# One max and one subtraction for two layers, and a semantic product in 32-row tiles: two cross-attention layers on one Trainium2 core

## The chip, the cores and the metric

The kernel runs on one NeuronCore of a Trainium2 chip. The metric is device time in microseconds (us), and less is better. All data are fp32. The engines are TensorE (PE; its weight loads are shown apart as PEld), VectorE (DVE), ScalarE (ACT), GpSimd (POOL) and SyncE (SP), which issues nearly all DMAs.

## The reference

Two cross-attention layers follow each other over 64 batch rows of 256 tokens and 320 channels, with 20 heads of 16 channels. The context has 77 rows of 512 channels; in layer 1 the last four of them are image rows. Cut to what matters:

```python
# layer 0: ip is empty (TEXT_LEN = 77)
q, k, v = split_heads(x @ Wq.T), split_heads(ctx @ Wk.T), split_heads(ctx @ Wv.T)
x = x + (softmax(q k^T / 4) v) @ Wo.T + bo

# layer 1: 73 text rows, 4 image rows
probs_t  = softmax(q k_t^T / 4)                       # [b, h, s, 73]
text_out = probs_t @ v_t
qsem     = l2norm(probs_t @ text_rows)                # 512 channels per head and token
sem      = qsem @ l2norm(ip_rows)^T                   # [b, h, s, 4]
probs_ip = softmax(q k_ip^T / 4 + 0.5 * sem) * spatial_mask
x = x + (text_out + probs_ip @ v_ip) @ W_out + b_out
```

## The kernel before

**No 512-channel intermediate.** With unnormalized weights w of layer 1, the kernel uses the Gram matrix G of the context rows. One product of w with [G | G times the image rows | values | 1] gives, for a head and a token, 94 columns: 73 of w G, 4 image sums, 16 text outputs and the sum of w. The squared norm of qsem is then w times (w G), summed. This is the *semantic product* (`semantics`, L774 and L781).

**Units.** The batch rows are taken in pairs p (32 pairs). A pair has ten units: for each of its two rows b five units, each of which is eight head slots of 128 tokens (four quarters r of 32 channels, two heads e in each). The main loop runs over g; g // 10 is p and g % 10 is k, the place in the pair. In one g, layer 0's scores of unit g and layer 1's scores of unit g - 13 are made, and the semantic product of the layer 1 unit of the g before. Layer 1 of a row thus runs while layer 0 of the next pair does. 307 values of g have both layers, the first 13 layer 0 alone and the last 13 layer 1 alone; 320 have a semantic product.

**One PSUM tile per g.** `ps` (tag `sc`) takes four of the eight PSUM banks, one bank for each quarter r, in one buffer. A bank holds layer 0's scores, layer 1's scores and the semantic product. So the first matmul of the next g (L774) waits until everything of this g has been read out of `ps`.

**The order inside one g,** as each engine gets it. PE, ACT, DVE and POOL keep the order in which the program is written (`keep_order`, from g = 13 on):

1. evictions of query or output projections held from the g before (`drains`): ACT L602 or L945, DVE L617; then PE: semantic product (L774, L781), scores of both layers (L659);
2. `shifted` for layer 0, then for layer 1: DVE max over the text (L677), DVE subtraction into `w` (L679);
3. `transposed(1)` of the g before: PE L723, L724; ACT L730, L731;
4. `exponential(0)`: ACT L687 on layer 0's `w`, except at k = 5, where it stands behind step 7;
5. DVE `weighted` (L792, L795): the semantic product times the weights;
6. `first` fillers: key, value or output projections, the Gram matrix and others, with their evictions on ACT (L348 `kT`, L391 `vs`, L516 and L517 `gram`, L589 `q`);
7. `transposed(0)` of the g before: PE L723, L724; ACT L749, L750, or L738, L741 in the last unit of a row;
8. `sums_out` (ACT L1057): the remaining 21 columns out of `ps`; at k = 1 and 6 it stands ahead of step 7;
9. `exponential(1)`: ACT L690, L691, and POOL L694, which copies the image scores from `w`; `normalize`: DVE L705, L706, POOL L710;
10. DVE L1130 and, at the end of a row, a chain of small steps (L870, L871, L844 and others);
11. `second` fillers, `attend` at four of the ten k (PE L809, L814, at k = 0, 2, 5, 7), `third` fillers.

Small PSUM tiles come from two pools of two buffers each: `ptr` (tag `tr`: transposes, `itr` L915, `ltr`, one `pv`) and `pms` (tag `ms`: projections, keys, values, Gram, the other `pv`). A matmul into such a tile waits until ACT or DVE has emptied the tile that had the buffer before it.

**The right-hand side of the semantic product.** `gv[b]` holds, for three channel groups and four blocks, G's first 64 rows twice (two halves of 64 partitions) and the values beside it; `gr[b]` holds the remaining nine rows in four quarters. `gram` fills `gram` and `g_rest` with one and eight DMAs, `place_gram` (POOL L530, L534) copies them into place. `values` fetches value rows from DRAM (`v_rows`) by DMA, `place_values` (POOL L435, L441, L449, L455 for layer 1; L464, L470, L475 for layer 0) places them.

Of the kernel before, what the change touches and what calls it, by code (L numbers as in the profile page):

```python
# [21 lines left out]
TT = T - NIP  # L22
P = 128
# [47 lines left out]
def tile_two_cross_attentions(ctx: ExitStack, tc: tile.TileContext, a: dict, out: bass.AP):  # L71
# [202 lines left out]
    gv = [const.tile([P, 3, 4, GV], F32, tag=f"gv{b}", name=f"gv{b}") for b in range(2)]  # L274
    gr = [const.tile([P, 3, 2, GR], F32, tag=f"gr{b}", name=f"gr{b}") for b in range(2)]
    for b in range(2):
        nc.vector.memset(gv[b][:, :, :, GV - 1 :], 1.0)
        nc.vector.memset(gr[b], 0.0)
        nc.gpsimd.tensor_copy(
            gr[b][:, :, :, GR - 1 :], rest1.unsqueeze(1).unsqueeze(3).broadcast_to([P, 3, 2, 1])  # L280
        )
# [5 lines left out]
    v_rest = [const.tile([P, C], F32, tag=f"v_rest{b}", name=f"v_rest{b}") for b in range(2)]  # L287
# [3 lines left out]
    parts1 = [const.tile([P, 5, 2, M], F32, tag=f"parts1{i}", name=f"parts1{i}") for i in range(3)]  # L291
# [45 lines left out]
    def keys(l, p, i):  # L337

        nt = (T, TT)[l]
        if i == 0:  # L340
            kTs[l] = big.tile([P, 2, 2, T], F32, tag=f"kT{l}", name=f"kT{l}_{p}", bufs=1)
# [8 lines left out]
    def last_keys(p):  # L350
# [5 lines left out]
        for l in range(2):  # L356
            nt = (T, TT)[l]
            kl = kls[l, p] = big.tile([P, 2, T], F32, tag=f"kl{l}", name=f"kl{l}_{p}", bufs=1 + l)
# [6 lines left out]
    def place_image_keys(p):  # L365

        k = kipT[:, :, 2 * p * NIP : 2 * (p + 1) * NIP].rearrange("p i (b t) -> p i b t", b=2)
        nc.gpsimd.tensor_copy(kTs[1][:, :, :, TT:], k[:, :2])
        nc.gpsimd.tensor_copy(kls[1, p][:, :, TT:], k[:, 2])

    def keys_by_head(l, p, b):

        kbd = kbds[l, b] = big.tile([P, 3, 2, T], F32, tag=f"kbd{l}", name=f"kbd{l}_{p}_{b}")
        for i, k in ((slice(0, 2), kTs[l][:, :, b, :]), (slice(2, 3), kls[l, p][:, b : b + 1, :])):
            full = [P, k.shape[1], 2, T]
# [7 lines left out]
    def value_rows(i, l):  # L383
# [8 lines left out]
        if l:  # L392
            v_rows[i] = dram.tile([P, 2, C], F32, tag="v_rows", name=f"v_rows{i}", bufs=8)
            nc.sync.dma_start(v_rows[i][:n], stage[i][:n])
# [3 lines left out]
    def from_rows(to, l, p, b, t0, t1):  # L398
# [3 lines left out]
        while at < end:  # L402
            i, r = divmod(at, P)
            n = min(P - r, end - at)
            o = at - r0 - t0
            nc.sync.dma_start(to[o : o + n, :], v_rows[i][r : r + n, l, :])
# [6 lines left out]
    def values(l, p, b):  # L413

        nt = (T, TT)[l]
        rem = nt - M
        vm = small.tile([P, C], F32, tag="vm", name=f"vm{l}_{p}_{b}", bufs=1)
        vr = v_rest[b] if l else small.tile([8 * rem, C], F32, tag="vr", name=f"vr{p}_{b}", bufs=1)
        for e in range(2):
            from_rows(vm[e * M : (e + 1) * M, :], l, p, b, 0, M)  # L420
        for i in range(8):
            r = i // 2 * QR + i % 2 * rem if l else i * rem
            from_rows(vr[r : r + rem, :], l, p, b, M, nt)
        fetched[l] = (vm, vr)

    def place_values(l, p, b):
# [3 lines left out]
        if l:  # L430

            for j in range(2):
                rows = slice(j * M, (j + 1) * M)
                for part in range(2):
                    nc.gpsimd.tensor_copy(  # L435
                        gv[b][rows, part, :, T : T + D].rearrange("p (e a) d -> p e a d", e=2),
                        vm[rows, 8 * D * part : 8 * D * (part + 1)].rearrange(
                            "p (a j e d) -> p j e a d", a=2, j=2, e=2
                        )[:, j],
                    )  # L440
                nc.gpsimd.tensor_copy(  # L441
                    gv[b][rows, 2, :, T : T + D].rearrange("p (e a) d -> p e a d", e=2),
                    vm[rows, HT * D + j * QR : HT * D + (j + 1) * QR]
                    .rearrange("p (e d) -> p e d", e=2).unsqueeze(2).broadcast_to([M, 2, 2, D]),
                )
            for r in range(4):
                rows = slice(r * QR, (r + 1) * QR)
                full = [QR, 2, 2, D]
                nc.gpsimd.tensor_tensor(  # L449
                    gr[b][rows, :2, :, T - M : T - M + D],  # L450
                    vr[rows, : HT * D].rearrange("p (i r e d) -> p r i e d", i=2, r=4, e=2)[:, r],
                    rest1[rows].unsqueeze(1).unsqueeze(3).broadcast_to(full), ALU.mult,
                )
                c0 = HT * D + r % 2 * QR
                nc.gpsimd.tensor_tensor(  # L455
                    gr[b][rows, 2, :, T - M : T - M + D], vr[rows, c0 : c0 + QR].rearrange("p (e d) -> p e d", e=2),
                    rest1[rows].unsqueeze(2).broadcast_to([QR, 2, D]), ALU.mult,
                )
# [42 lines left out]
    grams = {}  # L501

    def gram(p, b):
# [10 lines left out]
        g = small.tile([P, T], F32, tag="gram", name=f"gram{p}_{b}", bufs=2)  # L514
# [6 lines left out]
        nc.sync.dma_start(g[M:, :], g[:M, :])  # L521
# [4 lines left out]
        grams[b] = g  # L526

    def place_gram(b):
        g, gx = grams[b], g_rest[b]
        nc.gpsimd.tensor_copy(  # L530
            gv[b][:, :, :, :T], g.unsqueeze(1).unsqueeze(1).broadcast_to([P, 3, 4, T])
        )
# [116 lines left out]
    SEM0 = 4 * T  # L649

    def scores(ps, start, stop, l, p, b, u):
# [4 lines left out]
        for r in range(4):  # L656
            rows = slice(r * QR, (r + 1) * QR)
            for c in halves_of(P):
                nc.tensor.matmul(  # L659
                    ps[c, r, 2 * T * l : 2 * T * (l + 1)], tokens[rows, c],  # L660
                    kbd[rows, part].rearrange("p e t -> p (e t)"), start=start, stop=stop,
                )

    def shifted(ps, l, p, b, u):

# [538 lines left out]
```

## Time and profile before

| | |
|---|---|
| Time of three runs | median 2474.22 us (2473.43 to 2474.65) |
| Profiled execution | 2474.45 us, span 2472.7 us |
| Granted TensorE clock | 0.999 |
| Busy | PE 97%, PEld 75%, DVE 80%, ACT 60%, POOL 55% |
| DMA | 131.83 MB in 150914 packets, mean 53 GB/s |
| First and last semantic product | 114.9 us and 2444.0 us into the span |
| `L677` max, layer 0 / layer 1 | 796 / 756 ns each, x320 each |
| `L679` subtraction | 800 ns, x640 |
| `L774` semantic product, 64x64 tiles, 94 columns | 277.9 us busy, x10240 |
| `L659` scores, 32x64 tiles, 154 columns | 247.7 us busy, x10240 |

The profile shows one execution. An fp32 matmul is recorded as two matmul instructions, so a unit's 16 matmuls of L774 are 32 records. Matmuls on different tiles of the array overlap, and the time of a group is therefore the union of its records. The idle time given beside a row is the engine's idle time just before it, with whoever ended most of it. PE being busy includes matmuls that stand behind one another.

### The profile page before, as it was taken

The numbers are of one execution on the slowest core, as the hardware profiler recorded it, in microseconds if no ns is written. First come the engines' busy times: TensorE is split into PE (matmuls) and PEld (weight loads), VectorE is DVE, ScalarE is ACT, GpSimd is POOL, SyncE is SP. The second block draws the span as 40 slices with busy tenths as digits, with TensorE's granted clock in tenths as the row PEclk, the third lists the DMA queues.
The fourth block names the chain that finished last, engine by engine and source line by source line (L and its number), as shares of the span: only waits on it lengthen the run. The fifth ranks groups of instructions, "written<-read, shape, count | busy, mean of one in ns | idle before, by whom it ended". The sixth has DMA issues, their size and how long they took to land.

```text
span 2472.7 us, 100470 instructions
## 1 busy us (share of the span) xinstructions
PE 2394.2 (97%) x41118; PEld 1847.9 (75%) x41118; DVE 1987.4 (80%) x3673; ACT 1482.2 (60%) x3767; POOL 1370.9 (55%) x3483
## 2 busy tenths in 40 slices
PE   7899999999999999999999999999999999999888
PEld 5677777777777777777777777777777777777676
DVE  3588788888888888888888888888888888888864
ACT  3466666666666666666665666665665666666543
POOL 2455565566555656555656555556555556555542
PEclk9999999999999999999999999999999999999999
DMA  6212111112111112111121211121211121211000
GB/s 173 75 30 57 50 52 47 56 53 58 52 57 41 54 54 59 52 52 51 47 59 56 62 45 48 46 60 56 62 44 48 47 59 56 61 39 39 26 23 25
DMA packets 150914, 131.83 MB, mean 53 GB/s; under 512 B 45432, under 2 KB 129144, under 8 KB 150456
## 3 DMA queue, kind: packets, MB, share of 16 engines
q1 hardware_dynamic: 149592, 124.27, 17.5%
q8 instruction: 325, 5.32, 0.9%
q10 hardware_dynamic: 864, 1.15, 0.2%
q14 instruction: 133, 1.09, 0.1%
HBM read 87.43 MB, written 33.91 MB: 49 GB/s over the span
## 4 chain that ended last, share of the span: by engine, by line
PE 76%; DVE 12%; ACT 3%; DMA 3%; POOL 2%; issue 1%; SPq 1%; DVEq 0%; POOLq 0%; ACTq 0%
PE tr L723 10%; PE sc L774 9%; PE o_ps L547 8%; PE q_ps L547 8%; PE sc L659 7%; DVE w L679 5%; PE v_ps L390 4%; PE sc L781 4%; PE o_ps L632 3%; DVE mx L677 3%; PE k_ps L345 3%; PE pv L809 2%; PE q_ps L557 2%; PE o_ps L557 2%; PE q_ps L575 2%; PE pv L814 2%
## 5 line engine op out<-in xcount | busy, mean ns | idle before, releaser
L677 DVE TENSOR_REDUCE mx<-sc 128x8 f32<-128x584 f32 (+1 forms) x640 | 496.6, 776 | 342.1 <-PE sc L659 339.3
L710 POOL TENSOR_TENSOR parts<-w,sm 128x512 f32<-128x512 f32 (+1 forms) x640 | 440.6, 709 | 437.1 <-DVE sm L706 144.2
L679 DVE TENSOR_TENSOR w<-sc,mx 128x616 f32<-128x616 f32 x640 | 511.8, 800 | 73.0 <-DVE mx L677 1.4
L723 PE MATMUL tr<-ident,parts 128*128 128x128 f32 x2560 | 407.5, 282 | 9.5 <-ACT pt L730 5.6
L730 ACT COPY pt<-tr 128x512 f32<-128x512 f32 x320 | 187.1, 585 | 323.8 <-PE tr L723 318.9
L723 PEld LDWEIGHTS tr<-ident,parts 128*128 128x128 f32 x2560 | 284.2, 140 | 128.6 <-issue 83.1
L687 ACT ACTIVATE w<-w 128x616 f32<-128x616 f32 x320 | 230.1, 719 | 143.7 <-DVE w L679 142.7
L774 PEld LDWEIGHTS sc<-gv,pt 64*64 64x64 f32 x10240 | 233.5, 133 | 105.6 <-ACT sums L1057 52.7
L774 PE MATMUL sc<-gv,pt 64*64 64x94 f32 x10240 | 277.9, 245 | 23.6 <-ACT sums L1057 23.0
L694 POOL COPY att<-w 128x32 f32<-128x32 f32 x320 | 67.0, 209 | 354.6 <-DVE w L679 350.8
L705 DVE TENSOR_REDUCE sm<-w 128x8 f32<-128x616 f32 x320 | 250.9, 784 | 13.9 <-ACT w L687 13.8
L659 PE MATMUL sc<-kbd,q 32*64 32x154 f32 x10240 | 247.7, 293 | 1.1 <-ACT q L602 1.0
L547 PE MATMUL q_ps<-x,wq 128*128 128x256 f32 x1024 | 232.9, 380 | 5.3 <-ACT kT L348 5.3
L547 PE MATMUL o_ps<-aT,wo 128*128 128x256 f32 x1024 | 231.8, 379 | 0.7 <-ACT aT L945 0.7
L1057 ACT COPY sums<-sc 128x168 f32<-128x168 f32 x320 | 96.2, 301 | 225.8 <-DVE prod L795 223.9
L1130 DVE TENSOR_REDUCE nrm<-prod 128x8 f32<-128x584 f32 x320 | 226.7, 709 | 0.3
L792 DVE TENSOR_TENSOR prod<-sc,parts 128x512 f32<-128x512 f32 x320 | 217.9, 681 | 2.8 <-PE sc L781 2.8
L547 PEld LDWEIGHTS q_ps<-x,wq 128*128 128x128 f32 x1024 | 189.2, 190 | 30.2 <-ACT kT L348 7.3
L547 PEld LDWEIGHTS o_ps<-aT,wo 128*128 128x128 f32 x1024 | 189.6, 190 | 24.4 <-ACT aT L945 1.1
L690 ACT ACTIVATE parts<-w 128x512 f32<-128x512 f32 x320 | 206.4, 645 | 0.0
L749 ACT COPY pt<-tr 128x512 f32<-128x512 f32 x256 | 150.3, 587 | 66.9 <-PE tr L723 65.5
L390 PE MATMUL v_ps<-wv,cf 128*128 128x320 f32 (+1 forms) x624 | 179.2, 433 | 0.0
(144 smaller groups left out, 4560.3 us busy)
## 6 DMA issues: line engine op xcount, KB each, us to landing
out_dram<-x SPq DMA_DIRECT2D x64, 256.0 KB
x<-in_x_dram SPq DMA_DIRECT2D x31, 512.0 KB
v_rows<-vs SPq DMA_DIRECT2D x38, 320.0 KB
vm<-v_rows SPq DMA_DIRECT2D x152, 80.0 KB
ct<-in_ctx_dram SPq DMA_DIRECT2D x32, 308.0 KB
cf<-in_ctx_dram SPq DMA_DIRECT2D x38, 256.0 KB
g_rest<-gram_rest SPq DMA_DIRECT2D x512, 0.5 KB
v_rest<-v_rows SPq DMA_DIRECT2D x448, 11.2 KB
```

The lines of the kernel that those rows point to most:

```text
L390: nc.tensor.matmul(ps[:n, :C], cfs[i][:, k, :n], wv[l][:, k, :], start=(k == 0), stop=(k == KE - 1))
L547: nc.tensor.matmul(ps[b][:, m, :], w[:, k, m * P : (m + 1) * P], main[:, k, b * S : (b + 1) * S], start=(k == 0 and m == 0), stop=False,)
L659: nc.tensor.matmul(ps[c, r, 2 * T * l : 2 * T * (l + 1)], tokens[rows, c], kbd[rows, part].rearrange("p e t -> p (e t)"), start=start, sto ...
L677: nc.vector.tensor_reduce(mx, sc[:, :, :, :nt], AX.X, ALU.max)
L679: nc.vector.tensor_tensor(w, sc, mx.unsqueeze(3).broadcast_to([P, 4, 2, T]), ALU.subtract)
L687: nc.scalar.activation(w, w, AF.Exp, scale=SCALE)
L705: nc.vector.tensor_reduce(sm, w, AX.X, ALU.add)
L710: nc.gpsimd.tensor_tensor(two[:, 8 * t0 : 8 * t1].rearrange("p (h t) -> p h t", h=8), w[:, :, t0:t1], sm.unsqueeze(2).broadcast_to([P, 8, ...
L723: nc.tensor.transpose(ps[:, i, :], flat[:, i * P : (i + 1) * P], ident)
L774: nc.tensor.matmul(ps[c, i % 2 * 2 + j, at : at + GV], pt[half_rows, i, c], gv[b][half_rows, part, i, :], start=start and i < 2, stop=False,)
L792: nc.vector.tensor_tensor(prod[:, :, :, :M], sm[:, :, :, :M], w[:, :4].rearrange("p (e a) j t -> p (a j) e t", e=2), ALU.mult)
L1130: nc.vector.tensor_reduce(eight(stats[q, b][2], u), prod, AX.X, ALU.add)
```

## The change

Four edits go together.

- **Semantic product by quarters.** The weights of layer 1 are laid out by quarter: a 128-column transpose block holds 32 context rows of four quarters. `semantics` then makes 32 matmuls of 32x64 tiles in place of 16 of 64x64 tiles. G is symmetric, so the second half of a head (rows 32 to 63) skips the first 32 columns: 16 matmuls have 94 columns and 16 have 62. The off-diagonal block of G is doubled for it. `gv` is filled in quarters; `gq` and `vq` are new staging tiles.
- **One max and one subtraction.** In the 307 values of g with both layers, `shifted` makes one DVE max (16 outputs) and one DVE subtraction (1232 columns) over both layers' heads, in place of two of each. The image scores no longer lie inside layer 1's 77 columns: its four last text columns repeat its first four, and the image scores follow, so that layer 1's score matmul has 162 columns.
- **Image scores behind the sums.** ACT copies the image scores out of `ps` (32 columns) after `sums_out`; POOL's copy L694 is gone.
- **The sums' place.** `sums_out` with the copy stands ahead of `transposed(0)` at k = 1, 4, 6 and 9, and behind it otherwise.

```diff
-            full = [P, k.shape[1], 2, T]
+            full = [P, k.shape[1], 2, n]        # n = 77 in layer 0, 81 in layer 1
...
     def values(l, p, b):
-        for e in range(2):
-            from_rows(vm[e * M : (e + 1) * M, :], l, p, b, 0, M)
-        for i in range(8):
-            r = i // 2 * QR + i % 2 * rem if l else i * rem
-            from_rows(vr[r : r + rem, :], l, p, b, M, nt)
+        if l:
+            vm = small.tile([P, 2, 3, QR], F32, tag="vq", name=f"vq{p}_{b}", bufs=1)
+            vr = v_rest[b]
+            by_quarter = lambda rows: rows[:, C:].rearrange("t (i r c) -> r t i c", i=3, r=4)
+            for h in range(2):
+                for o, n, rows in pieces(p, b, h * QR, (h + 1) * QR):
+                    for r in range(4):
+                        nc.sync.dma_start(vm[r * QR + o : r * QR + o + n, h], by_quarter(rows)[r])
...
     def gram(p, b):
-        nc.sync.dma_start(g[M:, :], g[:M, :])
+        nc.gpsimd.tensor_scalar_mul(g[:QR, QR:M], g[:QR, QR:M], 2.0)
+        for r in range(4):
+            for h in range(2):
+                nc.sync.dma_start(gq[b][r * QR : (r + 1) * QR, h, h * QR :], g[h * QR : (h + 1) * QR, h * QR :])
...
-    def shifted(ps, l, p, b, u):
-        sc = ps[:, :, 2 * T * l : 2 * T * (l + 1)].rearrange("p r (e t) -> p r e t", t=T)
-        mx = small.tile([P, 4, 2], F32, tag="mx", name=f"mx{name}")
-        nc.vector.tensor_reduce(mx, sc[:, :, :, :nt], AX.X, ALU.max)
-        w = ws[l] = sp.tile([P, 4, 2, T], F32, tag=f"w{l}", name=f"w{name}", bufs=2 - l)
-        nc.vector.tensor_tensor(
-            w, sc, mx.unsqueeze(3).broadcast_to([P, 4, 2, T]), ALU.subtract
-        )
+    def shifted(ps, g, now):
+        h0, h1 = (0 if now[0] else 2), (4 if now[1] else 2)
+        full = [P, 4, h1 - h0, T]
+        sc = by_head_block(ps)[:, :, h0:h1, :T]
+        mx = small.tile([P, 4, 4], F32, tag="mx", name=f"mx{g}")[:, :, h0:h1]
+        w = sp.tile([P, 4, 4, T], F32, tag="w", name=f"w{g}")
+        nc.vector.tensor_reduce(mx, sc, AX.X, ALU.max)
+        nc.vector.tensor_tensor(w[:, :, h0:h1], sc, mx.unsqueeze(3).broadcast_to(full), ALU.subtract)
+        for l in range(2):
+            ws[l] = w[:, :, 2 * l : 2 * l + 2]
+
+    def image_scores_out(ps, p, b, u):
+        nc.scalar.copy(eight(stats[p, b][0], u), by_head_block(ps)[:, :, 2:, T:])
...
-        nc.gpsimd.tensor_copy(eight(stats[p, b][0], u), w[:, :, :, TT:])
...
     def semantics(ps, start, stop, p, b, u, rows):
         for i in range(4):
-            for j in range(2):
-                half_rows = slice(j * M, (j + 1) * M)
-                at = SEM0 + i // 2 * GV
+            e, h = divmod(i, 2)
+            at = slice(SEM0 + e * GV + h * QR, SEM0 + (e + 1) * GV)
+            for r in range(4):
+                quarter = slice(r * QR, (r + 1) * QR)
                 for c in halves_of(P):
                     nc.tensor.matmul(
-                        ps[c, i % 2 * 2 + j, at : at + GV], pt[half_rows, i, c], gv[b][half_rows, part, i, :],
-                        start=start and i < 2, stop=False,
+                        ps[c, r, at], pt[quarter, i, c], gv[b][quarter, h, part, e, h * QR :],
+                        start=start and i == 0, stop=False,
                     )
...
-        for l in range(2):
-            if now[l]:
-                shifted(ps, l, *now[l])
+        if now[0] or now[1]:
+            shifted(ps, g, now)
...
-        if before1 and k in (1, 6):
-            sums_out(ps)
+        if k in (1, 4, 6, 9):
+            taken(ps, now[1])          # sums_out, then image_scores_out
...
-        if before1 and k not in (1, 6):
-            sums_out(ps)
+        if k not in (1, 4, 6, 9):
+            taken(ps, now[1])
```

## The prediction

> **What bounds the kernel now.** I read the page first, for the load and the chain.
>
> ```profile
> PE 2394.2 (97%) x41118; PEld 1847.9 (75%) x41118; DVE 1987.4 (80%) x3673; ACT 1482.2 (60%) x3767; POOL 1370.9 (55%) x3483
> PE 76%; DVE 12%; ACT 3%; DMA 3%; POOL 2%; issue 1%; SPq 1%; DVEq 0%; POOLq 0%; ACTq 0%
> ```
>
> PE is full and carries three quarters of the chain. The share is an average over ten kinds of unit, so I then read one pair in the chain in order of time. Most units are PE from end to end. Two of them (k = 5 and 6) run through the other engines; this is k = 5:
>
> ```profile
> 1218.28 0.65 PE sc L774 x32
> 1218.93 0.30 PE sc L781 x16
> 1219.23 0.61 PE sc L659 x32
> ...
> 1219.86 0.81 DVE mx L677
> ...
> 1220.77 0.80 DVE w L679
> 1221.57 0.68 DVE mx L677
> ...
> 1222.37 0.80 DVE w L679
> 1223.17 0.60 DVE prod L792
> 1223.77 0.15 DVE prod L795
> ...
> 1223.94 0.31 ACT sums L1057
> ...
> 1224.29 0.88 PE sc L774 x32
> ```
>
> Here PE waits for `ps` to be read out. Third view, the waits of PE and its weight loads (total us, times, longest):
>
> ```profile
> PE sc L774 <- ACT sums L1057: 23.0, 55, 1.6
> PEld pv L809 <- ACT gram_rest L517: 6.1, 29, 0.6
> PEld itr L915 <- ACT pt L749: 4.9, 21, 1.1
> ```
>
> The last two are small, but they occur in nearly every pair: at k = 0 and k = 7 an eviction by ACT arrives exactly when PE wants it, with nothing to spare. What stands ahead of them on ACT is seen in the timeline of ACT at k = 7 (start, us):
>
> ```profile
> 1234.31 0.72 ACT L687 ACTIVATE w<-w 128x616 f32<-128x616 f32 x1 [0.37 <-DVE w L679]
> 1234.93 0.27 ACT L348 COPY kT<-k_ps 128x154 f32<-128x154 f32 x1
> 1235.10 0.59 ACT L749 COPY pt<-tr 128x512 f32<-128x512 f32 x1
> ```
>
> The exponential of layer 0 waits for DVE, and the evictions queue behind it. PE's L915 starts at 1235.74, when L749 ends at 1235.69.
>
> I cost the change unit by unit in the pair from 1201.0 to 1273.8. From the timeline, units start (first L774) at 1201.00 (k = 3), 1209.88, 1218.10, 1224.29, 1230.77, 1237.55, 1244.77, 1252.23 (k = 0), 1259.46, 1266.74, and the next k = 3 at 1273.80.
>
> **The semantic product on PE.** Over the trace's single records, the first L774 to the first L659 takes 962 ns. Eight rounds of four 64x64 tiles start 114, then 81 ns apart (94 columns); the change of tile shape to L781 costs 190; L781's two rounds of eight start 103 apart, and 59 pass to L659, whose rounds (154 columns, eight tiles) start 131 apart. After, there are four rounds of eight at 94 columns and four at 62, all in the 32x64 shape. By those spacings: 114 + 3 x 81 + 4 x 58 for L774, 58 + 60 for L781, no change of shape: 707 ns. Layer 1's scores have 162 columns for 154, 2 x 7 ns more. Net 0.24 us less a unit. Bounds: streaming alone (131/154 = 0.85 ns a column) would save 0.29. The nearest row the other way is L781 in the chain, 0.30 us for 16: 64 would take 1.20 for the 0.81 of L774, and with 0.13 for the drain that goes, a unit is 0.26 longer. I take 0.24, because L659 holds eight tiles in flight in just this shape and order.
>
> Eight neighbouring records of L659 or L781 start 6.7 ns apart. Against this stands the Trainium skill, "TensorE: Matmul & The Clock Gate", section "Wait — 56ns, not 53.3ns?": starts never come closer than about 25 ns, however few columns. By that rule the 80 matmuls of a unit would need about 2.0 us, 1.0 more than now; the records are already closer, so the sum goes by them.
>
> **Max and subtraction.** L677 takes 796 (616 columns) and 756 ns, L679 800; L792 and L795 give 1.04 ns a column (681 for 512, 223 for 72), so about 155 ns of each are fixed. Merged, over 1232 columns: 1.44 + 0.10 gap + 1.44 = 2.98 us, where the four took 3.30 (1219.86 to 1223.17). DVE gains 0.32 us. But layer 0's exponential needed only the first pair: it could start 1.70 us after the max began, and now 2.98. **It starts 1.28 us later**, and ACT works in order.
>
> **ACT's copy.** 585 ns for 512 columns and 273 for 128 give 195 for 32 (the small copies L516 and L517, 190 and 164 ns, bound it from below; 273 is above). It overlaps L1057 by 0.10, so `ps` comes free 0.09 us later.
>
> **Unit by unit** (T = unit's start, M = start of the max). M is T + 1.81 before where PE binds, T + 1.57 after.
> - k = 5: the exponential already stands behind the evictions. M + 2.98, product 0.74, sums and copy 0.39, hops 0.09: 5.77 for 6.19, **-0.42**. PE's own work (5.85 - 0.24) fits.
> - k = 6: the same with L890 between: 6.09 for 6.48, **-0.39**.
> - k = 7: M is bound by L902 and falls only to T + 1.69. Exponential ends T + 5.43, L348, then L749 ends T + 6.08. L915 starts at 6.13 (was 4.97), and 1.81 more to the end: 7.94 for 6.78, **+1.16**.
> - k = 8: L391, then L749, ends T + 6.11; `ltr` (L928) takes that transpose's buffer, 1.38 more: 7.5 for 7.22. In one pair of five a second value projection covers it (-0.24): **+0.20**.
> - k = 0: M follows DVE's small steps, T + 2.5 (was 2.71). Exponential ends T + 6.25, L516, L517 end 6.41; L809 starts 6.45 (was 5.36), 1.87 more: 8.3 for 7.23, **+1.05**.
> - k = 2: M is bound by four L617, T + 1.81. L749 can start at 5.45 and ends 6.04; L809 needs it: 6.09 (was 5.47), 1.59 more: 7.68 for 7.06, **+0.62**.
> - k = 4: L348 comes at T + 5.43; the second half of L547 wants its buffer at 5.25: **-0.03**.
> - k = 1, 3, 9: PE has long projections meanwhile and nothing waits: **-0.24** each.
>
> The pair's sum: -0.42 - 0.39 + 1.16 + 0.20 + 1.05 + 0.62 - 0.03 - 0.72 = +1.47 us.
>
> **Costed at nothing.** POOL loses L694 (320 x 209 ns), and per row its 14 small L435, L441, L449 and L455 become two; it has slack now (437.1 us of idle time ahead of L710, 1.4 a unit), so that this is worth nothing on the path. SP issues about 925 more DMAs of 0.3 to 0.75 us (rows L406 and L525) to 2673 that take 1.31 ms: 65 to 80% of its time. The tightest place is the Gram at k = 0: sixteen issues in a row for nine (1258.17 to 1264.92). At 0.67 us each and 0.7 to land, the last is there near 1269.6, where POOL's L534 started at 1268.87, with `keys_by_head` behind it, and L710 only at 1274.06. Some 2 us of POOL's idle time cover it; without them PE's L659 at k = 3 would wait up to 2 us a pair.
>
> **The sum.** 307 units have both layers: 30.7 x 1.47 = +45. The 13 last units have layer 1 alone and save some 0.2 each: -3. 2474.45 + 42 gives about 2517 us; the execution stands 0.2 us above the median.
>
> **The rivals.**
> - *Faster: the evictions have room* (0.21). If PE is not held at k = 0, 2, 7, 8, each of those saves 0.24 too: eight units x 0.24 and 0.81 for k = 5, 6 make 2.7 us a pair, about 86 in all: 2389. For it speaks that ACT is busy only 60%. Against it, L915 and L809 already wait for exactly these evictions. It decides if the delay of L687 is under about 0.85 us instead of 1.28; the sum crosses zero near there, since 1.47 is spread over three to four stalls.
> - *Slower by issue* (0.10): the 80 matmuls run at L781's 0.30 us for 16 on top of the stalls: 0.50 x 320 = 160 more, 2677.
> - *SP late* (0.05): Gram and value DMAs miss POOL, up to 2 us in 31 pairs: 2580.
> - *The two effects cancel* (0.06): stalls a third smaller: within 5 us of 2474.
>
> **How the numbers follow.** My forecast has 0.58. Its own range, 2485 to 2550, takes stalls 0.2 us off in each of four units (25 us) and the product between 0.29 and 0.15. The range for eight in ten is wider, 2440 to 2590: it takes in the cancelling case, SP, and half stalls, and leaves out the fully faster and the issue-bound ends. A measurement tells about 0.2%, 5 us. Faster: the 0.21 and a little of the cancelling case and of my own, 0.24. Same: 0.04. Slower: 0.72.
>
> **What would show it.** In the new profile the rounds of the semantic product should start 81 and 58 ns apart and the max come at T + 1.57. The exponential of layer 0 should start 3.0 us after the max. L915 (k = 7) and L809 (k = 0 and 2) should show PE waiting 0.6 to 1.3 us for ACT's `pt` or `gram_rest`; k = 7 should last near 7.9 us, k = 0 near 8.3, k = 5 near 5.8. I am wrong if PE still has no idle time at those places, if L780's matmuls start further than 10 ns apart, or if POOL waits for DMAs of `gq` or `vq`.

## The result, and the profile after

The changed kernel takes 2615.61 us (median of four runs, 2612.34 to 2621.78) against 2474.43 us: a ratio of 1.0573, 95% interval 1.0551 to 1.0596. It is 141 us slower, where the prediction said 42. The profiled execution took 2613.27 us, with a span of 2611.6 us at a granted clock of 0.993 (0.999 before).

The page, load and chain:

```profile
PE 2445.4 (94%) x51358; PEld 1892.0 (72%) x51358; DVE 1952.3 (75%) x3059; ACT 1494.4 (57%) x4087; POOL 1178.2 (45%) x2587
PE 57%; DVE 19%; ACT 8%; SPq 6%; POOL 4%; DMA 3%; issue 3%; ACTq 0%; DVEq 0%; POOLq 0%
```

PE's share of the chain falls from 76% to 57%. DVE has 35 us less to do and carries more of the chain (19% for 12%), and SP's queue, at 1% before, now carries 6%. So PE waits more, for two different things. The chain at k = 5 (start, length; this unit starts at 1283.55):

```profile
1283.62 0.82 PE sc L780 x49
...
1284.73 0.61 PE sc L657 x30
...
1285.36 1.45 DVE mx L679
...
1286.91 1.45 DVE w L680
...
1288.38 0.72 ACT w L691
```

One max and one subtraction in a row, as costed. But the max starts 1.81 us after the unit's first product, and not at 1.57. Before, it started 1.76 us after it at this k (1219.86 against 1218.10 in the chain above), and 1.82 in the median of all k, which is also the median after. PE's product saved nothing here. At k = 2 it even starts late. PE's timeline at its start, before (1266.4 to 1266.75) and after (1257.7 to 1258.13):

```profile
1266.09 0.83 PE L557 MATMUL o_ps<-aT,wo 64*64 64x256 f32 x12
1266.74 0.25 PE L774 MATMUL sc<-gv,pt 64*64 64x94 f32 x2
```

```profile
1257.36 0.83 PE L555 MATMUL o_ps<-aT,wo 64*64 64x256 f32 x12
1258.12 0.30 PE L780 MATMUL sc<-gv,pt 32*64 32x94 f32 x2
```

Behind the same twelve matmuls on 64x64 tiles, the product starts 0.65 us after the first of them before, and 0.76 after. The stalls are next. ACT's timeline at k = 7 of the same pair (the unit starts at 1295.79), and PE's:

```profile
1300.57 0.72 ACT L691 ACTIVATE w<-w 128x616 f32<-128x616 f32 x1 [1.61 <-DVE w L680]
1301.19 0.27 ACT L350 COPY kT<-k_ps 128x154 f32<-128x154 f32 x1
1301.36 0.59 ACT L754 COPY pt<-tr 128x512 f32<-128x512 f32 x1
```

```profile
1299.71 1.22 PE L357 MATMUL kl_ps<-ct,wk_last 128*128 128x154 f32 x8
1302.00 0.63 PE L921 MATMUL itr<-ident,iw 128*80 128x128 f32 x4 [1.07 <-ACT pt L754]
```

This is the foreseen stall: ACT idles 1.61 us for the subtraction, the eviction L754 queues behind the exponential, and PE stands idle for 1.07 us. The waits of PE, its loads and POOL (total us, times, longest):

```profile
POOL gr L532 <- DMA g_rest<-gram_rest: 110.8, 29, 5.4
...
PE pv L815 <- ACT gram_rest L510: 36.2, 29, 1.4
PE itr L921 <- ACT pt L754: 32.2, 30, 2.1
...
PE pv L815 <- ACT pt L754: 13.4, 32, 1.1
...
PE sc L657 <- POOL kbd L380: 12.5, 10, 4.5
```

Three of these four waits of PE are the stalls of k = 0, 7 and 2, once in every pair. The first line had been priced at nothing: POOL waits for the Gram's DMAs in nearly every pair, and ten times PE's scores wait for POOL after it.

The granted clock is half in nine stretches of 3.4 or 6.8 us, 37.5 us in all (two and 6.8 us before); in them the transposes of L728 start 213 ns apart where 109 is usual. Even if everything in them ran at half rate, this costs some 15 us more than before, so it can't be the main cause of the 141.

The windows between two semantic products, by place in the pair (difference of the means over all pairs, us), beside the prediction and the run with the merge alone (e2 below). In the code, the product made in a g belongs to the layer 1 unit whose scores were made two g before, so the first one is at g = 15.

| k | 1 | 2 | 3 | 4 | 5 | 6 | 7 | 8 | 9 | 0 | sum |
|---|---|---|---|---|---|---|---|---|---|---|---|
| predicted | -0.24 | +0.62 | -0.24 | -0.03 | -0.42 | -0.39 | +1.16 | +0.20 | -0.24 | +1.05 | +1.47 |
| after | +0.24 | +0.60 | +0.65 | +0.27 | -0.13 | -0.15 | +1.16 | +0.57 | -0.04 | +1.10 | +4.27 |
| merge alone | 0.00 | +0.57 | +0.01 | +0.21 | -0.31 | -0.24 | +1.13 | +0.54 | -0.02 | +1.06 | +2.97 |

### The profile page after: what moved, and what is told of

It is laid out like the page before. It is cut to its first block, busy times and chain, and to the rows that moved or that the text cites. A ratio compares the mean times of both kernels' runs of the same rounds, so it can differ in the third digit from the quotient of the medians.

```text
span 2611.6 us, 120325 instructions
## 1 busy us (share of the span) xinstructions
PE 2445.4 (94%) x51358; PEld 1892.0 (72%) x51358; DVE 1952.3 (75%) x3059; ACT 1494.4 (57%) x4087; POOL 1178.2 (45%) x2587
## 3 DMA queue, kind: packets, MB, share of 16 engines
q10 hardware_dynamic: 864, 1.15, 0.1%
## 4 chain that ended last, share of the span: by engine, by line
PE 57%; DVE 19%; ACT 8%; SPq 6%; POOL 4%; DMA 3%; issue 3%; ACTq 0%; DVEq 0%; POOLq 0%
PE sc L780 9%; DVE w L680 8%; PE q_ps L545 8%; DVE mx L679 8%; PE sc L657 6%; PE o_ps L545 6%; PE tr L728 5%; ACT w L691 3%; PE v_ps L394 3%; PE pv L815 3%; PE q_ps L555 2%; SPq L426 2%; PE pv L820 2%; PE sc L787 2%; PE k_ps L347 2%
## 5 line engine op out<-in xcount | busy, mean ns | idle before, releaser
L679 DVE TENSOR_REDUCE mx<-sc 128x16 f32<-128x1232 f32 (+1 forms) x333 | 462.5, 1389 | 538.5 <-PE sc L657 534.4
L680 DVE TENSOR_TENSOR w<-sc,mx 128x1232 f32<-128x1232 f32 (+1 forms) x333 | 463.4, 1392 | 30.6 <-DVE mx L679 0.9
L728 PE MATMUL tr<-ident,parts 128*128 128x128 f32 x2560 | 409.4, 283 | 10.9 <-ACT pt L735 5.5
L735 ACT COPY pt<-tr 128x512 f32<-128x512 f32 x320 | 187.4, 586 | 390.6 <-PE tr L728 390.6
L728 PEld LDWEIGHTS tr<-ident,parts 128*128 128x128 f32 x2560 | 285.3, 141 | 134.9 <-issue 83.9
L780 PEld LDWEIGHTS sc<-gv,pt 32*64 32x64 f32 x20480 | 276.3, 131 | 122.7 <-issue 46.8
L780 PE MATMUL sc<-gv,pt 32*64 32x94 f32 (+1 forms) x20480 | 319.8, 240 | 17.8 <-ACT att L685 16.0
L657 PE MATMUL sc<-kbd,q 32*64 32x154 f32 (+1 forms) x10240 | 288.2, 303 | 15.5 <-POOL kbd L380 12.5
L545 PE MATMUL q_ps<-x,wq 128*128 128x256 f32 x1024 | 239.7, 382 | 1.0
L694 ACT ACTIVATE parts<-w 128x512 f32<-128x512 f32 x320 | 212.3, 664 | 0.0
L657 PEld LDWEIGHTS sc<-kbd,q 32*64 32x64 f32 x10240 | 184.9, 130 | 25.1 <-POOL kbd L380 15.7
L729 PE MATMUL rtr<-ident,parts 128*104 128x128 f32 (+1 forms) x640 | 175.2, 274 | 0.0
L787 PE MATMUL sc<-gr,pr 32*64 32x60 f32 x5120 | 166.8, 234 | 0.0
```

The source lines that it names most:

```text
L545: nc.tensor.matmul(ps[b][:, m, :], w[:, k, m * P : (m + 1) * P], main[:, k, b * S : (b + 1) * S], start=(k == 0 and m == 0), stop=False,)
L657: nc.tensor.matmul(by_head_block(ps)[c, r, 2 * l : 2 * l + 2, : kbd.shape[3]], tokens[rows, c], kbd[rows, part], start=start, stop=stop,)
L679: nc.vector.tensor_reduce(mx, sc, AX.X, ALU.max)
L680: nc.vector.tensor_tensor(w[:, :, h0:h1], sc, mx.unsqueeze(3).broadcast_to(full), ALU.subtract)
L728: nc.tensor.transpose(ps[:, i, :], flat[:, i * P : (i + 1) * P], ident)
L780: nc.tensor.matmul(ps[c, r, at], pt[quarter, i, c], gv[b][quarter, h, part, e, h * QR :], start=start and i == 0, stop=False,)
```

## The experiments

Three theories were to be told apart. A: the merged subtraction delays the exponential, and the evictions behind it stall PE. S: the product by quarters saves PE nothing, because past a first burst pairs of weight load and matmul (one record of each) come some 15 ns apart, whatever their columns. D: the further DMAs come late and cost time by themselves. Each result is the median of four executions (two for e8); "before" ran beside it each time at 2474 to 2477 us.

| run | what | us | ratio to before, 95% |
|---|---|---|---|
| e1 | after, exponential moved | 2566.59 | 1.0378 (1.0350 to 1.0407) |
| e2 | before + merge | 2565.83 | 1.0370 (1.0355 to 1.0386) |
| e3 | after without the merge | 2583.05 | 1.0439 (1.0421 to 1.0458) |
| e4 | after, 94 columns throughout | 2622.17 | 1.0602 (1.0580 to 1.0623) |
| e5 | before + gq's DMAs | 2515.09 | 1.0159 (1.0141 to 1.0177) |
| e6, e13 | e1 + keys first, run twice | 2520.00, 2530.89 | 1.0178 (1.0161 to 1.0195), 1.0222 (1.0201 to 1.0243) |
| e7 | before + merge, exponential moved | 2454.43 | 0.9911 (0.9897 to 0.9926) |
| e8 | after, half the product | 2541.67 | 1.0264 (1.0243 to 1.0284) |
| e9 | e6, k = 4 moved too | 2549.78 | 1.0305 (1.0290 to 1.0321) |
| e10 | e9 without gq's DMAs | 2535.26 | 1.0242 (1.0227 to 1.0257) |
| e11 | e9, tiles not split | 2552.18 | 1.0309 (1.0294 to 1.0325) |
| e12 | e7, tiles not split | 2565.49 | 1.0366 (1.0349 to 1.0383) |
| e14 | e2, scores first | 2656.63 | 1.0729 (1.0711 to 1.0747) |
| e15 | e6 without gq's and vq's DMAs | 2502.99 | 1.0114 (1.0096 to 1.0132) |

### The delayed exponential: e2, e1, e3, e7

e2 puts the max and subtraction over both layers (77 columns each, no other edit) into the kernel before.

```diff
-        for l in range(2):
-            if now[l]:
-                shifted(ps, l, *now[l])
+        if now[0] or now[1]:
+            shifted(ps, g, now)      # one max, one subtraction
...
```

> The kernel before with the merged max and subtraction alone (both layers, 77 columns a head, so that layer 1's max also runs over its image scores, which changes no softmax). Product, DMAs, POOL's copy and the sums' place as before. Theory A: the exponential starts 1.28 us later; k = 0 +1.2, k = 2 +0.85, k = 7 +1.25, k = 8 +0.4, k = 4 +0.2, k = 5 and 6 -0.32 each: +3.3 us a pair, 2575 us. Theory B: only DVE's gain shows, k = 5 and 6 -0.32 each: 2455 us.

Measured: 2565.83 us, as theory A had it. In this run's waits the stalls stand with the sizes that they have in the changed kernel:

```profile
PE itr L914 <- ACT pt L748: 36.3, 30, 2.2
PE pv L808 <- ACT gram_rest L517: 36.2, 29, 1.6
...
PE pv L808 <- ACT pt L748: 17.0, 32, 1.2
```

So the edit that takes 39 us of work off DVE (busy 1948.3 us for 1987.4) costs 91 us. e1 goes the other way: the changed kernel with the exponential behind the evictions.

```diff
-        if now[0] and k != 5:
+        if now[0] and k not in (0, 2, 5, 7, 8):
             exponential(0, g, *now[0])
...
-        if now[0] and k == 5:
+        if now[0] and k in (0, 2, 5, 7, 8):
             exponential(0, g, *now[0])
```

> The changed kernel with one edit: layer 0's exponential is queued on ACT behind the evictions of transposed(0) at k = 0, 2, 5, 7, 8 instead of at k = 5 alone. Theory A (evictions held up behind the exponential that waits for the merged subtraction): PE's waits ahead of L815 (k = 0 and 2), L921 (k = 7) and L934 (k = 8), about 4 us a pair in the changed kernel, go; the units become about 7.3, 7.1, 6.9 and 7.3 us for 8.32, 7.68, 7.80 and 7.92, in all 3.1 us a pair or 95 us: 2520 us. Theory B (the loss is the semantic product and the DMAs, and PE's waits are only its visible end): less than 20 us are won, 2595 or more.

Measured: 2566.59 us, between the two. The stalls went as theory A said (k = 0, 2, 7, 8 at 7.02, 7.18, 6.97 and 7.35 us for 8.32, 7.67, 7.80 and 7.92), but k = 3 rose from 9.03 to 9.90 us (mean 10.82, single ones up to 17.7). One of them shows where the time went. SP, POOL and PE:

```profile
2214.31 0.83 SPq L521 DMA_DIRECT2D g_rest<-gram_rest  x1
2215.24 5.86 SPq L517 DMA_DIRECT2D gq<-gram  x8
2221.14 5.24 SPq L521 DMA_DIRECT2D g_rest<-gram_rest  x7
```

```profile
2229.49 0.32 POOL L532 TENSOR_TENSOR gr<-g_rest,rest 128x78 f32<-128x78 f32 x1 [5.58 <-DMA g_rest<-gram_rest]
...
2231.51 0.46 POOL L380 TENSOR_TENSOR kbd<-kl,head_mask 128x162 f32<-128x162 f32 x1
```

```profile
2232.02 0.85 PE L657 MATMUL sc<-kbd,q 32*64 32x162 f32 x16 [4.63 <-POOL kbd L380]
```

The sixteen issues of the Gram take 12.07 us, the last lands 3.1 us after its issue, POOL waits 5.58 us with the keys by head queued behind it, and PE waits 4.63 us for those keys. Without the stalls, PE reaches this point earlier and the DMAs do not. Over the run PE's L657 waits 36.0 us for these keys, 20 times, where the changed kernel has 12.5 in 10. The clock adds to it: it is half in fourteen stretches, 52 us in all, seven of them in units k = 3 right behind a wait of PE of 1.7 to 6.2 us. e3 undoes the merge alone in the changed kernel.

```diff
+        for l in range(2):
+            sc = by_head_block(ps)[:, :, 2 * l : 2 * l + 2, :T]
...
+            nc.vector.tensor_reduce(mx, sc, AX.X, ALU.max)
+            nc.vector.tensor_tensor(w, sc, mx.unsqueeze(3).broadcast_to([P, 4, 2, T]), ALU.subtract)
```

> The changed kernel with the max and subtraction made layer by layer again; product by quarters, DMAs, ACT's copy and the sums' place stay. Theory A: no PE wait for gram_rest, pt or vs; the units of k = 0, 2, 7, 8 are within 0.15 us of before; what is left is ACT's copy (0.09 at k = 5 and 6), the product (+0.05 a unit or less) and late DMAs at k = 3 (0.4 a pair): 2474 + 25 to 40, about 2505 us. Theory B: the product and DMAs hold the loss, above 2580 us.

Measured: 2583.05 us: the stalls went (k = 0, 2, 7 at 7.23, 7.17, 6.99 us) and k = 3 rose to 9.62 (mean 10.59), with the same wait of L657 for the keys (30.3 us, 18 times). A alone is refuted as the whole cause, as its own number (2505) was missed by 78 us; the second cost covers what the first gave up. The costs do not add: the stalls hide late DMAs. e7 then asks whether the merge is good when its exponential no longer stands in the way. It is e2 with e1's edit, with k = 4 in the list as well.

> The kernel before with the merged max and subtraction alone, and layer 0's exponential behind transposed(0) at k = 0, 2, 4, 5, 7, 8. If the merge costs only through the evictions that stand behind the exponential: k = 0, 2, 7, 8 return to 7.0, 7.1, 6.9, 7.3 us, k = 5 and 6 keep 5.87 and 6.15, and the time is 2455 to 2470 us, 5 to 20 below before. If the later max-dependent work costs elsewhere too (layer 1's exponential, the sums that free the PSUM tile), it stays above 2485.

Measured: 2454.43 us, 22 less than before (interval 0.9897 to 0.9926) and 111 less than e2, with k = 0, 2, 7 and 8 at 6.91, 7.06, 6.80 and 7.22 us. Its page:

```profile
PE 2390.4 (97%) x41118; PEld 1851.9 (76%) x41118; DVE 1939.8 (79%) x3059; ACT 1475.9 (60%) x3767; POOL 1370.8 (56%) x3483
PE 87%; ACT 4%; DVE 3%; DMA 2%; POOL 2%; issue 1%; SPq 0%; POOLq 0%; ACTq 0%; DVEq 0%
```

The chain is PE to 87%. This is the version that beats both kernels.

### The product by quarters: e4, e8, e11, e12

e4 gives all 32 matmuls 94 columns, the first 32 of each second half being zeros.

```diff
-            at = slice(SEM0 + e * GV + h * QR, SEM0 + (e + 1) * GV)
+            at = slice(SEM0 + e * GV, SEM0 + (e + 1) * GV)
...
-                        ps[c, r, at], pt[quarter, i, c], gv[b][quarter, h, part, e, h * QR :],
+                        ps[c, r, at], pt[quarter, i, c], gv[b][quarter, h, part, e, :],
```

> The changed kernel with 94 columns in all 32 matmuls of the product (the second halves get zeros in their first 32 columns, the result is the same). Theory S (supply: after some 34 pairs of weight load and matmul, PE gets a pair each 16.7 ns, whatever the columns): the first product matmul to the first score matmul stays at 0.91 us within 0.05, the time within 10 us of 2615. Theory C (columns: a round of eight takes 81 ns at 94 columns and 58 at 62): four rounds 23 ns longer, 0.09 us a unit, M from 1.81 to 1.90, about 2640 us.

Measured: 2622.17 us, and the first score again 0.911 us after the first product. Half as many columns again (94 for 62) in half of the matmuls cost next to nothing (the max came 0.03 us later), so columns did not set the pace. In the median over all units of the changed kernel the 32nd pair starts 0.314 us after the first, in four rounds of eight within which pairs start 6.7 ns apart; the other 80 take 1.15 us, 14.6 ns each. e8 leaves the second-half products out (`for i in (0, 2)` in place of `range(4)`).

> The changed kernel without the second-half products (it leaves out the 16 matmuls of 62 columns of each unit, half of G and of the values; 80 records ahead of the first score become 48). If the supply of weight-load and matmul pairs sets the pace (16.7 ns each past the first forty), the first product to the first score falls from 0.909 to about 0.40 us, and the units that PE binds (k = 1, 3, 9) by 0.5. If streaming sets it (four rounds of 58 ns less), it falls to about 0.68, and the units by 0.2. The time is then near 2540 by the first and near 2590 by the second, if the stalls at k = 0, 2, 7, 8 stay as long as before.

Measured: 0.523 us to the first score, between the two, and k = 1 and 9 shorter than in the changed kernel by 0.36 and 0.34 us. Streaming (0.68) is refuted. The supply theory is off in its size: the burst was taken as forty pairs, and it ends at 32 or 33 in the changed kernel and in e8. In the median over e8's units the 32nd pair starts at 0.344 us and the 80th and last at 1.119, 16.1 ns each.

e11 and e12 halve the number of pairs the other way, with tiles that are not split into column halves (`halves_of(P)` becomes one slice of 128 in product, rest and scores).

> The kernel of the first run of this call, with product, rest and scores on 32x128 tiles (no split of the 128 columns): 56 pairs of weight load and matmul in a unit for 112. Supply theory: the first product to the first score falls from 0.909 to about 0.45 us, the max starts at T + 1.4 instead of T + 1.81, and the time falls by 30 to 70 us. Streaming theory (a tile of 128 columns takes twice the time of one of 64, or four tiles in flight take what eight took): the first score comes at 0.9 us or later, the max at T + 1.8 or later, and the time does not fall.

> The kernel before with the merge and the late exponential (2454 us), with product, rest and scores unsplit (64x128 and 32x128 tiles): 40 pairs in a unit for 80. Supply theory: its 64x64 rounds (81 ns for four pairs) were not bound by supply, so the product keeps its 0.64 us; the gap of 0.17 us to the rest stays; the scores (131 ns for eight pairs, 16.4 each) could be bound by either. So the max comes between T + 1.4 and T + 1.81, and the time is 2410 to 2455 us. Streaming theory: T + 1.8 or later, 2454 us or more.

Measured: 2552.18 us against 2549.78 for e9, and 2565.49 against 2454.43 for e7. The supply theory's forecast failed in both. With unsplit tiles the first score comes later (1.162 us for 0.911, and 1.332 for 0.973) and the max at T + 2.00 and T + 2.16. The single records show another limit: rounds of unsplit tiles with 94 columns start 111 ns apart, where the kernel before has 81 for the same work in halves. The split is worth 111 us to the kernel of e7. So the pace past the burst is measured, and that columns do not set it (e4); what in PE sets it is not shown.

### The further DMAs: e5, e6, e9, e10, e15

e5 adds only the eight issues of `gq`, read by nobody, to the kernel before.

```diff
         nc.sync.dma_start(g[M:, :], g[:M, :])
+        for r in range(4):
+            for h in range(2):
+                nc.sync.dma_start(gq[b][r * QR : (r + 1) * QR, h, h * QR :], g[h * QR : (h + 1) * QR, h * QR :])
```

> The kernel before, with the eight further DMAs of gq issued ahead of g_rest's eight (their target is read by nobody). SP's issuing goes from 39.5 to about 50 us in a pair of some 80, and the run of issues at k = 0 from nine to seventeen. Theory D (late DMAs cost on their own): POOL's L534 waits for g_rest some 30 times, 2 to 4 us each, the keys by head come late, PE's scores at k = 3 wait, k = 3 goes from 8.88 us to between 9.3 and 10, and the time to 2490 to 2525 us. Rival (the Gram's issues cost nothing on their own; what remained in the runs with the merge undone comes from the product's shape or the value DMAs): within 6 us of 2474, k = 3 at 8.9.

Measured: 2515.09 us, 38 more, by eight further DMAs a row. The tile `gq` is made by a line left out above. The place differs from the expected one: k = 3 keeps its median of 8.88 us (mean 9.15), and k = 4 takes most (mean 9.22 for 8.36). The waits say why:

```profile
POOL gr L538 <- DMA g_rest<-gram_rest: 106.6, 30, 6.0
...
POOL v L464 <- DMA vm<-v_rows: 63.8, 18, 7.2
...
ACT kT L348 <- POOL kbd L376: 32.6, 12, 4.8
...
PE q_ps L551 <- ACT kT L348: 20.9, 10, 3.8
```

The values of layer 0 stand behind the Gram in SP's queue and come late too; POOL's keys come late behind them, and ACT's eviction into the single buffer `kT` waits until POOL has read it, and PE's L551 waits for that eviction. e6 tests the order on POOL: e1 with the keys by head written ahead of `place_gram`.

```diff
-            add(1, p - 1, place_gram, 0)
             add(1, p, keys_by_head, 0, p, 1)
             add(1, p - 1, keys_by_head, 1, p - 1, 0)
+            add(1, p - 1, place_gram, 0)
```

> The changed kernel with layer 0's exponential behind transposed(0) at k = 0, 2, 5, 7, 8 (as in the first run of this study, 2567 us), and with the keys by head written ahead of place_gram at k = 1 and k = 8. If POOL's wait for g_rest is what delays PE's scores at k = 3, k = 3 goes from 9.90 us (mean 10.82) to about 9.1 (mean below 9.5), and the time to 2520 to 2535 us. If the delay comes from something else on the way (values of layer 0, loads of x), k = 3 keeps a mean above 10.3 and the time stays within 10 us of 2567.

Measured: 2520.00 us, 47 less than e1, with k = 3 back at 9.03 us (mean 9.12). POOL still waits for `g_rest` (64.6 us in all), but the keys no longer stand behind that wait, and PE's wait for them is gone (36.0 us in e1). This shows the path of e1's second cost, and e3 has the same wait. e9 adds k = 4 to the exponential's list in e6.

> The changed kernel with layer 0's exponential behind transposed(0) at k = 0, 2, 4, 5, 7, 8 and the keys by head ahead of place_gram at k = 1 and 8: the run of 2520 us with k = 4 added to the list. If the eviction behind the exponential still stalls PE at k = 4 there (8.72 us for 8.22 before), k = 4 falls to about 8.3 and the time to 2505 to 2510 us; if k = 4's length comes from late DMAs, both stay.

Measured: 2549.78 us, a loss of 30. k = 4 fell as expected (8.72 to 8.42), but k = 5 rose from 6.00 to 7.27:

```profile
PEld k_ps L347 <- ACT q L600: 41.6, 28, 1.6
...
PE k_ps L347 <- ACT q L600: 35.0, 28, 1.3
```

In the changed kernel the sums stand ahead of `transposed(0)` at k = 4, so an exponential behind both starts 6.47 us into the unit (4.85 in e7, where the sums stand last), and the next unit's evictions queue behind it. The same move that is free in one order costs 1.27 us in the other. e10 takes `gq`'s DMAs out of e9.

> The kernel of the run beside it (exponential late at six k, keys first), without the eight DMAs of gq in each row (it leaves G out of the main products). SP's issuing falls from 57 to about 46.5 us a pair. Theory D (SP's late issues are what remains of the loss): 25 to 45 us faster than the run beside it, 2465 to 2485 us, and the first semantic product 4 to 5 us earlier. Rival (what remains is the product's shape on PE): within 8 us of the run beside it.

Measured: 2535.26 us, 14.5 less, and the first product 4.7 us earlier. The gain lies between the two forecasts (25 to 45, and within 8). That the keys, written first, cover the rest of the lateness is likely but not shown. The run labelled e13 is e6's kernel once more, so its text does not describe it; it shows that this kernel's median moves by 11 us from one chip to another (2520.00 and 2530.89), and nothing more.

> The changed kernel with the exponential late at k = 0, 2, 5, 7, 8 and the keys first (2520 us), without the DMAs of gq and of vq (it leaves G and the values out of the main products; POOL clears vq instead): SP's issuing falls from 57 to about 40 us a pair, as before the change. What is left over the 2454 us of the kernel before with the merge made cheap is then the product by quarters itself. If PE's shape is that rest (a unit that PE binds 0.14 us longer, the product starting 0.1 us later behind a 128-row tile): k = 1 stays at 7.42 us, and the time is 2475 to 2500 us. If the DMAs are the rest: k = 1 falls to 7.3 and the time to 2450 to 2465 us.

e15 is the kernel that was meant (`gq`'s and `vq`'s `dma_start` left out of e6).

> The run labelled e13 was the same kernel as e6, a second time (2531 us on another chip, 2520 on the first); what e13's expectation describes is run here: the changed kernel with the exponential late at k = 0, 2, 5, 7, 8 and the keys first, without the DMAs of gq and of vq (it leaves G and the values out of the main products; POOL clears vq instead). If PE's shape is the rest of the loss over 2454 us: k = 1 stays at 7.42 us, and the time is 2475 to 2500 us. If the DMAs are the rest: k = 1 falls to 7.3 and the time to 2450 to 2465 us.

Measured: 2502.99 us: above the range of either theory, and k = 1 did not fall (7.55 us: the last score there starts 1.60 us into the unit, for 1.48 in e6; why is open). The chain of this run:

```profile
PE 81%; DVE 7%; POOL 5%; ACT 4%; issue 2%; DMA 1%; SPq 0%; ACTq 0%; DVEq 0%; POOLq 0%
```

SP is out of it, and 28 us over before remain. So the DMAs are worth 17 us against e6 and 28 against e13, which ran on the same chip as e15, once the order is right, and 49 us separate e15 from e7. Of those, k = 4 (mean 8.67 for 8.31, not in e15's list) makes 30.6 x 0.36 = 11. The other 38 us, 1.2 a pair, are left to the product by quarters, with its wider scores, ACT's copy and the sums' new places, which no run took apart. They are spread unevenly (k = 7 +0.46, k = 1 +0.32, k = 3 +0.13 in the means). All of k = 3 and 0.14 of k = 1 are explained below. Of k = 7 (14 us in all), 8.7 us are stops of PE that e7 does not have, most of them in this line of e15's waits:

```profile
PE sc L654 <- issue: 7.6, 8, 1.5
```

In e15 PE and its weight loads stand still together ten times for 0.3 us or more, 10.6 us in all, and the profile shows nothing that they wait for. The other kernels with 112 pairs in a unit that were counted (the changed kernel, e1, e3, e6, e9, e10, e13) have six to ten such stops, 4 to 12 us; those with 80 or fewer (before, e2, e5, e7, e11, e12) have none. The cause of the stops is open, and so is the rest of the 38 us.

### Scores first: e14

e14 is e2 with the scores ahead of the product in the list `todo`.

> The kernel before with the merged max and subtraction, and PE's scores written ahead of the semantic product, layer 0's exponential where it was. The merge alone cost 91 us because the exponential came 1.28 us later. With the scores first, the max can start some 1.2 us earlier in a unit and the exponential is back at about its old time. If the exponential's time is the whole cost of the merge, the stalls at k = 0, 2, 7, 8 go without moving the exponential, and the time is 2440 to 2475 us. If the product's late end (and with it the product of weights and sums, and the release of the PSUM tile) matters as well, or PE then waits for keys or queries that came just in time, it stays above 2490.

Measured: 2656.63 us, 91 more than e2. The lever did not act, so the run tells nothing on the exponential. The waits show it:

```profile
DVE mx L678 <- PE sc L780: 533.5, 283, 6.6
```

The max still waits for L780, the last matmul into the same PSUM tile, though it reads none of its columns. It starts 2.00 us after the first score, where it started 1.82 us after the first product: 0.18 us more for the same matmuls, whose tile shape changes twice in that stretch instead of once. That the second change is the reason is likely but not shown alone, and what else makes up the 91 us was not traced. (The 190 ns that the prediction read off the trace for a change of shape are from the start of one round to the start of the next, and an ordinary round takes 81 of them.)

## Why the prediction was right or wrong

- **The delayed exponential: right in mechanism, place and size.** It starts 4.83 us into a unit for 3.55, 1.28 later; max and subtraction take 2.99 us. k = 0, 2 and 7 last 8.32, 7.67 and 7.80 us for 8.3, 7.68 and 7.94 predicted. PE waits 1.18, 0.37 and 1.05 us a pair at L815, L815 and L921. The rival in which the evictions have room is refuted by e2, and the sign followed from it.
- **The semantic product, 0.24 us less a unit: this is the step that failed.** The first score starts 0.909 us after the first product, not 0.707, and the last at 1.475 for 1.446; the max comes at T + 1.81 in both kernels. Two readings were at fault. The sum took rounds of eight every 81 and 58 ns, 7 to 10 ns a pair, for all of the product; that pace held for 32 pairs, and the others came 14.6 ns apart. (L659's 131 ns for a round of eight was no such rate: in e12 a round has four pairs of the same 154 columns, and takes 131 ns too.) And the change of tile shape was counted as gone. It only moved: in the kernel before, the product's 64x64 tiles at k = 2, 4 and 5 follow L557's 64x64 tiles and start 196 ns after L557's last record; in the changed kernel 32x64 tiles follow it (L555 there) and start 306 ns after. That is 0.11 us (the Trainium skill, "TensorEngine Tiling (Array Packing)", section "Key Properties", says that changing the tiling mode drains the engine; it gives no price, and the rows agree), and 0.03 from the later last score, so k = 1 is 0.14 longer in the median (7.42 for 7.28) where 0.24 less was forecast; k = 3, which ends the same way, is 0.15 longer (9.03 for 8.88). Behind 128-row tiles, at k = 3's own start, the product starts 202 ns after the last record in both kernels.
- **What this step was worth.** The table above is short by 2.80 us a pair, 86 of the 98.6 us missed; 5 more are in the first product's later start (120.0 for 114.9 us), and the last 13 units took 2.9 us more instead of 3 less. Seven units (k = 1, 3, 4, 5, 6, 8, 9) carried the 0.24 in full, 1.68 of the 2.80; late DMAs at k = 3 are another 0.50 (next point), and the change of shape 0.11 each at k = 1, 3 and 4. k = 4 and 8, called -0.03 and +0.20, are among the seven: with the max at T + 1.81 their evictions come too late, and e2, with no product by quarters, has +0.21 and +0.54 there.
- **POOL and SP at nothing: wrong, but smaller.** The prediction named the right place (Gram, k = 0, then `keys_by_head`, then the scores at k = 3) and said that 2 us of POOL's idle time cover it. In the case shown (e1) the sixteen issues took 12.07 us, 0.75 each where it had 0.67, and the last landed 3.1 us later, not 0.7. In the changed kernel k = 3 has a mean 0.50 above its median: 15 us. The stalls at k = 0 and 2 give the DMAs time; without them (e1, e3) the same cause shows in full, 0.9 to 1.0 us more a pair by the means of k = 3 over their medians and another 0.6 to 0.9 in the medians.
- **The rule that was weighed.** By the rule of the Trainium skill's page "TensorE: Matmul & The Clock Gate", section "Wait — 56ns, not 53.3ns?" (starts no closer than about 25 ns), an estimate puts the unit's 80 product records at 2.0 us; they take 0.91. So the trace differs from the rule, and going by the trace was right. But the records quoted against it were those of a short burst; over the 112 pairs of the unit the trace lies between the two, at 13.3 ns a pair, and that would have put the saving near zero.
- **The rivals.** "Slower by issue" (2677) and "SP late" (2580) both came true in part, on top of the stalls. Each had been priced as if it came alone, and the range took in SP but cut off issue, which holds most of the miss.
- **ACT's copy: right.** It takes 202 ns in the mean, for 195, and PE's idle time ahead of L780 for it is 16.0 us in all, where 23.0 stood there for L1057 before.

The parts: merge +91 us (e2), what is left to the product some +38, DMAs 17 to 28 with the keys first; together 146 to 157 for the measured 141. That they overlap rather than add is shown by e1 and e3, so this sum is a check of size and no account of each part.

## What to carry to other kernels

Fusing two steps on one engine saves its busy time and delays the first result; look at what is queued in order behind the consumer of that result before counting the saving, and move the consumer with the fusion (e2 against e7: 111 us for five further places of one line). A spacing read from neighbouring records is a rate only over the length of the burst in which it was read; go by the n-th record of the whole stretch. A stall that is removed uncovers whatever it was hiding, so an engine whose queue is nearly full, here SP, should be priced with the stalls gone.

## What the runs showed of the hardware that was not expected

- Of the pairs of weight load and fp32 matmul on eight 32x64 tiles, the first 32 come in rounds of eight, 6.7 ns apart within a round, and take 0.314 us; the others start 14.6 ns apart on average (16.1 in e8), with 62 columns as with 94 (e4).
- Unsplit tiles with 94 columns start in rounds 111 ns apart, where two column halves take 81 (e12 against e7).
- A 32x64 product starts 0.11 us later behind 64x64 tiles than a 64x64 product does (306 ns for 196).
- The granted clock falls to half for 3.4 or 6.8 us behind some waits of PE (in e1's k = 3, of 1.7 to 6.2 us), and transposes then start 213 ns apart for 109 (L728, changed kernel).
- A DMA of nine partitions within SBUF takes SP 0.70 us (median) to issue at 0.5 KB, and eight more issues a row cost the kernel before 38 us (e5).
